# Spreading the four activations of a split piece over the steps, and putting GpSimd's reads of x2 first, in a two-layer convolution kernel

## The chip, the core and the metric

The kernel runs on one core of a Trainium2 chip. The metric is the device time of one execution in microseconds (us). Three runs of the kernel before gave 6400.53, 6409.91 and 6413.18 us, so its median is 6409.91 us. The profile comes from one more execution.

## The reference, cut to what matters

The input is four images of 96 channels and 128 x 128 pixels. A first layer (a state space scan) makes a new image `x`. The second layer, where the change lies, normalises each image and splits it at zero into a positive and a negative part:

```python
xr, x1, x2 = _relu_split_norm(x, sc1, sc2, res_coef, nc1, nc2)
y1 = NORM_SCALE * _layer_norm(_attn_conv(x1, x2, aw1, aw2, aw3))
y2 = NORM_SCALE * _layer_norm(_conv2d(x2, w_conv2, K // 2)) * x1
y = jnp.concatenate([y1, y2], axis=1)
return xr + _conv2d(y, w_full, 0) + b_full[None, :, None, None]
```

`_attn_conv` convolves x1 and x2 with 3 x 3 kernels into a key and a query, makes from their products (a softmax) the weights of one more 3 x 3 convolution per image, and applies it to a third convolution of x1, the value. All the images are independent in this layer.

## The kernel before, in words

**Stages.** Up to about 3600 us the first layer runs for all images, and image 0 passes its own split and its key, query, value and c2 convolutions (`direct_maps`, line 2126 on). After that, `attention` (line 1959) runs image by image on TensorE: for each strip of twelve rows it makes key, query, value and c2 (image 0 has them by then), then the attention weights (`weights`, line 1683), then the last convolution with those weights. This stream is called *left*. A second stream, *light*, prepares the next image and finishes the one before: `ssm_output`, then the split of image b+1, then `attn_output` of image b-1. `co_run` (line 302) pulls the two generators in turn by the costs that they yield, and so sets the order of emission.

**The order of the instructions.** In the stages after the scan nothing is pinned by hand: the Tile scheduler takes the emitted instructions, with their order of emission as priority, and writes one fixed order for each engine. Every engine then works through its own list in order. An instruction whose input is not there stops those behind it on its engine.

**The split.** `split_norm` (line 1101) reads an image in 16 pieces of 96 x 1024 pixels (tile `xn`). For images 1 to 3 (`planes` true) a piece has two sides, x1 and x2, and each side two halves of 512 pixels. For each half ScalarE writes scale*x + shift into a PSUM bank (line 1263), and VectorE multiplies it by the comparison of x with the threshold and writes it to SBUF, into the tile `half` (line 1267). The banks come from a pool of two that the light stream shares (`psr`), so the activation of one half can't start before VectorE has read the bank of two halves earlier.

**Steps.** `Later` (line 317) is a queue of closures with a count; each `tick` runs those whose count is 0 and lowers the others. A piece has six ticks, called steps here. Before, all four activations are emitted ahead of step 1, and the four VectorE operations in step 1. Then `planes_of` (line 1387) makes from each side six combinations of four neighbouring columns, the "planes", which the attention's Winograd-like products read. For x1 (`scaled`, line 1424) ScalarE makes two scaled copies, x4 (all columns, line 1428) and x2 (two column groups, line 1429; this x2 is a scratch tile, not the image part), in step 2; GpSimd combines them in ten operations (`differences`, line 1432, lines 1437 to 1442 and four of line 1406) in step 3; the store to memory (line 1450) is emitted in step 6. For x2 (`at_once`, line 1408) VectorE does it alone in step 5 with nine operations (lines 1413, 1414, 1418, two of 1420, four of 1406), and the store follows in step 6. The attention's value passes through the same `scaled` and `differences` (tile `own`), five or six rows at a time.

**Buffers.** x1 has two `half` tiles that alternate, x2 has one. In the split, x4 has two buffers and the scratch tile x2 one; the planes `pl` and `plv` have one each. `xn` has three.

**Other work named later.** Line 1477 and 1492 are the attention's matmuls; ScalarE copies their results out (`ends`, `odd`, line 1550), VectorE combines them (lines 1564 to 1572), and ScalarE copies shifted inputs (`yb`, line 1938) and transposed tiles (`kt`, line 1775). `weights` has the chain reduce (1697), exponential (1700), reciprocal and scaling (1701, 1702), transposes on TensorE (1711), copies (1712) and the combination of lines 1302 to 1308.

Of the kernel before, what the change touches and what calls it, by code (L numbers as in the profile page):

```python
# [11 lines left out]
AF = mybir.ActivationFunctionType  # L12
ALU = mybir.AluOpType
# [4 lines left out]
C = 96  # L18
# [14 lines left out]
TN = W // TW  # L33
# [38 lines left out]
def kernel(  # L72
# [26 lines left out]
    nc = tc.nc  # L99
# [193 lines left out]
    def part(ps, *shape):  # L293
        n = 1
        for d in shape[1:]:
            n *= d
        t = bank(ps)[: shape[0], :n]
        return t if len(shape) == 2 else t.rearrange("p (a b) -> p a b", b=shape[2])
# [802 lines left out]
    def split_norm(xnew, x1d, x2d, stats, keep, cnt, ps, side, planes, vector, done):  # L1101


        with ExitStack() as pools:
# [12 lines left out]
            a = col("rstd")  # L1117
            rsqrt(a, gs[:, 1:2])

            m = col("m1")  # L1120
# [19 lines left out]
            later = Later()  # L1140
# [58 lines left out]
            shift = kept[:, 0:2]  # L1199
            nc.vector.tensor_mul(shift, sa, navg)  # L1200
            scale = kept[:, 2:4]
# [18 lines left out]
            thr = kept[:, 8:9]  # L1220
# [4 lines left out]
            def stored(i, m, h):  # L1225
                if planes:
                    def then(pl):
                        store_planes(nc.sync, m, i * RS, RS, pl)
                        done[m is x2d] = (i + 1) * RS

                    return planes_of(later, p2, h, RS, then, vector=vector(i, m is x2d))
                at = (i * RS + 1) * PW
                return lambda: nc.scalar.dma_start(m[:, at : at + RS * PW], h)
# [8 lines left out]
            for i in range(NS):  # L1242
                y = ahead.pop(0)
                piece(i + 3)
                for side_, m in ((0, x1d), (1, x2d)):
                    op = ALU.is_le if side_ else ALU.is_gt
                    if planes:
                        h = half[side_][i % len(half[side_])]
                        v, to = (
                            t.rearrange("p (a b) -> p a b", b=b)[:, :, 0:TN]  # L1250
                            for t, b in ((y, TN), (h, PB))
                        )
                        k, parts = TW * R, 2
                    else:
                        h = p2.tile([C, RS * PW], F32, name=f"half{side_}", bufs=4)
                        hv = h.rearrange("p (h w) -> p h w", w=PW)
                        nc.gpsimd.memset(hv[:, :, 0:1], 0.0)
                        v, to = y.rearrange("p (h w) -> p h w", w=W), hv[:, :, 1:PW]
                        k, parts = RS, 1
                    for a in range(0, k * parts, k):  # L1260
                        x, o = v[:, a : a + k], to[:, a : a + k]
                        f = part(ps, C, k, TN) if planes else o
                        nc.scalar.activation(
                            f, x, AF.Identity,
                            scale=scale[:, side_ : side_ + 1], bias=shift[:, side_ : side_ + 1],
                        )
                        later(lambda o=o, x=x, f=f, op=op: nc.vector.scalar_tensor_tensor(
                            o, x, thr, f, op, ALU.mult
                        ))
                    later(stored(i, m, h), 1 + 3 * side_ * planes)  # L1270
                for _ in range(6 if planes else 1):
                    later.tick()
                    yield 2.5 if planes else 3.5
# [113 lines left out]
    def planes_of(later, pool, t, r, then, most=RS, vector=False, bufs=2, p=C, pb=PB, pp=PP):  # L1387

        a2 = AA * AA
        v = t[:, : r * pp].rearrange("p (h x) -> p h x", x=pp)
        over = pb - 1

        def planes(name, bufs):
            pl = pool.tile([128 if p < C else p, NP, most * TN], F32, name=name, bufs=bufs)[:p, :, : r * TN]
            return pl, [pl[:, i].rearrange("p (h t) -> p h t", t=TN) for i in range(NP)]

        def sums(eng, mid, outer, to):
            f1, f2 = mid[:, :, 0:TN], mid[:, :, pb : pb + TN]  # L1400
            f3, f0 = outer[:, :, 0:TN], outer[:, :, over:]
            for i, op, x, y in (
                (1, eng.tensor_add, f2, f1), (2, eng.tensor_sub, f2, f1),
                (0, eng.tensor_sub, f2, f0), (5, eng.tensor_sub, f3, f1),
            ):
                op(to[i], x, y)  # L1406

        def at_once():
            f = pool.tile([p, most, 6 * TN + 4], F32, name="diff", bufs=1)[:, :r]
            mid, outer, df = f[:, :, : 2 * PB], f[:, :, 2 * PB : 130], f[:, :, 130:]  # L1410
            pl, to = planes("plv", 1)
            stt = nc.vector.scalar_tensor_tensor
            stt(mid, v[:, :, : 2 * PB], -a2, v[:, :, 2 * PB :], ALU.mult, ALU.add)
            stt(
                outer, v[:, :, 2 * PB : 2 * PB + 2 * TN], -a2, v[:, :, 1 : 1 + 2 * TN],
                ALU.mult, ALU.add,
            )
            nc.vector.tensor_sub(df, v[:, :, 2 * PB :], v[:, :, : 2 * PB])
            for i, f in ((3, AA), (4, -AA)):
                stt(to[i], df[:, :, 0:TN], f, df[:, :, PB : PB + TN], ALU.mult, ALU.add)  # L1420
            sums(nc.vector, mid, outer, to)
            later(lambda: then(pl))

        def scaled():
            q = 128 if p < C else p
            x4 = pool.tile([q, most * JW], F32, name="x4", bufs=bufs)[:p, : r * pp]
            x2 = pool.tile([q, most, 2, PB], F32, name="x2", bufs=1)[:p, :r]
            nc.scalar.mul(x4, t[:, : r * pp], a2)
            nc.scalar.mul(x2, blocks(t, r, pp, 2 * pb, 2, PB), AA)
            later(lambda: differences(x4.rearrange("p (h x) -> p h x", x=pp), x2))  # L1430

        def differences(x4, x2):
            mid, outer = x4[:, :, : 2 * PB], x4[:, :, 2 * pb : 2 * pb + over + TN]
            d1 = x2[:, :, 0, 0:TN]
            pl, to = planes("pl", 1)
            sub, add = nc.gpsimd.tensor_sub, nc.gpsimd.tensor_add
            sub(mid, v[:, :, 2 * pb : 2 * pb + 2 * PB], mid)
            sub(outer, v[:, :, 1 : 1 + over + TN], outer)
            sub(to[4], v[:, :, 3 * pb : 3 * pb + TN], v[:, :, pb : pb + TN])
            sub(d1, x2[:, :, 1, 0:TN], d1)  # L1440
            add(to[3], to[4], d1)
            sub(to[4], to[4], d1)
            sums(nc.gpsimd, mid, outer, to)
            later(lambda: then(pl), 2)

        return at_once if vector else scaled
# [1075 lines left out]
    with tc.tile_pool(name="wp", bufs=1, side="left") as wp:  # L2522
# [7 lines left out]
        for images, pace in (([0], 0.25), ([1], 0.75), ([2, 3], 1.35)):  # L2530
            left = projections(images, weights, stats, wp, psl)
            if images[0] == 0:
                next(left)
                next(others)
                made = pair_weights()
                next(made)
                while ready[0] < 2:
# [3 lines left out]
                planes = [  # L2541
                    [new_planes(f"{n}{i}") for n in ("x1p", "x2p", "vp")] for i in range(2)
                ]
# [154 lines left out]
```

## Time and profile before

| what | value |
|---|---|
| median of three runs | 6409.91 us |
| the profiled execution | 6409.68 us |
| its span, first to last instruction | 6407.8 us, so 1.9 us lie around it |
| granted TensorE clock, mean | 0.902 |
| the split of image 1 | 3607 to about 3803 us, beside the end of image 0's maps and its last convolution |
| the split of image 2 | 4290 to 4570 us, beside the attention of image 1 |
| the split of image 3 | 5109 to 5405 us, beside the attention of image 2 |
| DMA, mean over the span | 188 GB/s |

The page of a profile gives for each engine its busy time and share. A view of windows gives the same for stretches of time. A line of the view of waits says who waited for whom: the sum in us, how often, the longest. A line of the timeline has the start in us, the duration in us, engine, line of the source, operation, output<-inputs, and in brackets the idle time of the engine before it with what ended it. PE is TensorE, PEld its weight loads, DVE VectorE, ACT ScalarE, POOL GpSimd; a q after the engine's name marks its sequencer, which waits or issues DMAs.

### The profile page before, as it was taken

Reading aid. Unit: us, or ns where it says so; the run is one execution under the profiler, and the core shown is the slowest. Engines: PE = TensorE matmul, PEld = TensorE weight load, DVE = VectorE, ACT = ScalarE, POOL = GpSimd, SP = SyncE. Lnnn points to the kernel's source line nnn. Section 1 sums busy time; section 2 is a strip of 40 time slices with the busy share of each in tenths; the row PEclk is TensorE's granted clock in tenths of the full one; section 3 lists DMA queues with packets and bytes.
Section 4 is the critical chain, followed back from the end, with each engine's and each line's share of the span. In section 5 each row is a group of like instructions: output and inputs, shape, how many; then the busy total and the mean of one; then the engine's idle time right before and its main releaser. Section 6 shows DMA issues by size and latency. Waiting matters only on the chain. (4 is left out here: it accounts for less than half of the span.)

```text
span 6407.8 us, 76468 instructions
## 1 busy us (share of the span) xinstructions
PE 5253.4 (82%) x23264; PEld 2254.8 (35%) x23264; DVE 4699.9 (73%) x7132; ACT 3759.4 (59%) x4770; POOL 3238.6 (51%) x2476
## 2 busy tenths in 40 slices
PE   6889988987888643989988588977888877889888
PEld 2333322322222111444433234345333444345553
DVE  4247878988989768989844686468774687988767
ACT  1247767787787666777622465466644665545642
POOL 1326757978879554979822234436304365022310
PEclk9899989998999765999999799989989888999989
DMA  6766777775675766676667686665776656967668
GB/s 155 175 160 189 198 199 199 214 221 163 198 202 171 202 183 207 196 213 179 182 185 195 166 228 163 195 169 156 214 199 184 175 149 165 245 167 180 191 168 221
DMA packets 897706, 1205.30 MB, mean 188 GB/s; under 512 B 230644, under 2 KB 745642, under 8 KB 884816
## 3 DMA queue, kind: packets, MB, share of 16 engines
q1 hardware_dynamic: 866640, 1145.36, 65.5%
q0 software_dynamic: 16336, 38.51, 2.3%
q10 hardware_dynamic: 14320, 16.54, 0.9%
q8 instruction: 187, 3.06, 0.2%
q14 instruction: 223, 1.83, 0.1%
HBM read 777.82 MB, written 345.62 MB: 175 GB/s over the span
## 5 line engine op out<-in xcount | busy, mean ns | idle before, releaser
L633 PE MATMUL bank<-y,wp 128*128 128x512 f32 (+3 forms) x3584 | 1310.9, 622 | 83.8 <-DMA y<-y 41.0
L866 POOL TENSOR_TENSOR y<-y,dl 128x1024 f32<-128x1024 f32 x384 | 1058.5, 2757 | 263.0 <-DVE dl L858 240.3
L833 POOL TENSOR_TENSOR dl<-dl,u 128x1024 f32<-128x1024 f32 x384 | 1008.8, 2627 | 253.1 <-ACT dA L809 121.1
L854 DVE TENSOR_TENSOR_SCAN dA<-dA,pBC 128x512 f32<-128x512 f32 x768 | 981.6, 1278 | 30.7
L2169 PE MATMUL bank<-y,wn 128*64 128x384 f32 (+5 forms) x2408 | 680.1, 507 | 58.3 <-DMA y<-x1d 34.1
L1477 PE MATMUL two<-ya,wd 128*64 128x192 f32 (+3 forms) x2376 | 582.2, 414 | 174.0 <-ACT odd L1550 65.1
L633 PEld LDWEIGHTS bank<-y,wp 128*128 128x128 f32 (+3 forms) x3584 | 456.2, 168 | 749.3 <-issue 651.1
L858 DVE TENSOR_TENSOR dl<-dA,pBC 128x512 f32<-128x512 f32 x768 | 528.5, 688 | 255.8 <-PE pBC L747 183.8
L747 PE MATMUL pBC<-xr,wbc 60*128 60x512 bf16 (+1 forms) x1536 | 457.8, 404 | 311.5 <-DVE dA L854 239.1
L1938 ACT COPY yb<-ya 64x768 f32<-64x768 f32 (+1 forms) x660 | 537.7, 815 | 195.5 <-PE two L1477 113.8
L676 ACT ACTIVATE dl<-pd,dtb 128x512 f32<-128x512 f32 x768 | 485.5, 684 | 187.9 <-PE pd L747 171.5
L1477 PE MATMUL two<-yb,wd 128*64 128x192 f32 (+3 forms) x2376 | 559.0, 400 | 4.0 <-ACT yb L1938 4.0
L837 DVE TENSOR_TENSOR pBC<-dl,pBC 128x512 f32<-128x512 f32 x768 | 527.5, 687 | 8.8 <-POOL dl L833 7.8
L2169 PEld LDWEIGHTS bank<-y,wn 128*64 128x64 f32 (+3 forms) x2408 | 310.3, 169 | 357.2 <-issue 186.2
L809 ACT ACTIVATE dA<-dl,negA 128x1024 f32<-128x1024 f32 x384 | 420.3, 1141 | 2.3
L1477 PEld LDWEIGHTS two<-ya,wd 128*64 128x64 f32 (+1 forms) x2376 | 262.2, 165 | 370.9 <-ACT odd L1550 75.0
L676 ACT ACT_TABLE_LOAD x248 | 318.2, 1283 | 91.9 <-PE pd L747 79.7
L747 PEld LDWEIGHTS <-wbc 60*128 60x128 bf16 (+1 forms) x1536 | 103.1, 96 | 752.1 <-issue 739.3
L1477 PEld LDWEIGHTS two<-yb,wd 128*64 128x64 f32 (+1 forms) x2376 | 289.7, 167 | 150.5 <-issue 42.1
L1477 PE MATMUL two<-ya,wa 128*96 128x384 f32 (+1 forms) x528 | 231.2, 521 | 72.9 <-DMA ya<-vp 27.0
L1550 ACT COPY odd<-two 128x384 f32<-128x384 f32 (+5 forms) x176 | 115.8, 658 | 291.3 <-PE two L1492 179.1
L1406 POOL TENSOR_TENSOR pl<-x 96x256 f32<-96x256 f32 (+3 forms) x396 | 275.2, 710 | 0.0
(322 smaller groups left out, 9105.4 us busy)
## 6 DMA issues: line engine op xcount, KB each, us to landing
u<-zb SPq DMA_DIRECT2D x192, 1024.0 KB
yms<-y SPq DMA_DIRECT2D x96, 512.0 KB
xn<-xnew SPq DMA_DIRECT2D x128, 384.0 KB
ya<-vp SPq DMA_DIRECT2D x120, 336.0 KB
y<-y SPq DMA_DIRECT2D x128, 258.2 KB
zb<-z SPq DMA_DIRECT2D x64, 512.0 KB
y<-yms SPq DMA_DIRECT2D x64, 512.0 KB
ya<-x1p SPq DMA_DIRECT2D x90, 336.0 KB
```

The costliest lines, as they stand in the source:

```text
L633: nc.tensor.matmul(blocks(pz[p:e]), lhsT=ws[k][:, d, c : c + e - p], rhs=window(ys[k], at, d, n), start=(i == 0), stop=(i == len(terms) - 1),)
L676: nc.scalar.activation(dst, src, AF.Softplus, bias=bias)
L747: nc.tensor.matmul(p, lhsT=w[rows], rhs=xr[rows, at : at + CH], start=True, stop=True)
L809: nc.scalar.activation(live[m]["dA"], live[m]["dl"], AF.Exp, scale=negA[:, g % 3, k : k + 1])
L833: nc.gpsimd.tensor_mul(t, t, u_view(n))
L837: nc.vector.tensor_mul(p, live[n]["dl"][:, bass.ts(half, CH)], p)
L854: nc.vector.tensor_tensor_scan(h, h, p, init, ALU.mult, ALU.add)
L858: nc.vector.tensor_mul(live[n]["dl"][:, sl], live[n]["dA"][:, sl], live[n]["C", half])
L866: nc.gpsimd.tensor_add(v, v, t.rearrange("p (a b) -> p a b", b=W))
L1477: nc.tensor.matmul(of(to[p:e], r), lhsT=w[:, i, c : c + e - p], rhs=tiles(t[k][PAIR[i]][:, SLOT[i]], o, r), start=(k == 0), stop=False,)
L1938: nc.scalar.copy(yb[k][64 * h - 64 : 64 * h, :, :n], ya[k][0:64, :, h * TN : h * TN + n])
L2169: nc.tensor.matmul(pc[p:e, :n].rearrange("p (h w) -> p h w", w=W), lhsT=w[:, c : c + e - p], rhs=v[:, :, 0:W], start=(i == 0), stop=(i == ...
```

## The change

In `split_norm` the activation of a half is put into a closure `made`. The first of a piece is emitted at once; the second, third and fourth are handed to `later`, so that they are emitted in steps 1, 2 and 3. Each closure queues its VectorE operation for the step after. The planes of x1 begin one step later (count 2 for 1), those of x2 in the same step as before (count 4). Image 0's split (`planes` false) has the turn 0 everywhere and keeps its order. In `differences` the same ten GpSimd operations are emitted in another order: the four that read the scratch tile x2 or feed those that do come first.

```diff
-                        f = part(ps, C, k, TN) if planes else o
-                        nc.scalar.activation(
-                            f, x, AF.Identity,
-                            scale=scale[:, side_ : side_ + 1], bias=shift[:, side_ : side_ + 1],
-                        )
-                        later(lambda o=o, x=x, f=f, op=op: nc.vector.scalar_tensor_tensor(
-                            o, x, thr, f, op, ALU.mult
-                        ))
-                    later(stored(i, m, h), 1 + 3 * side_ * planes)
+
+                        def made(x=x, o=o, op=op, side_=side_, k=k):
+                            f = part(ps, C, k, TN) if planes else o
+                            nc.scalar.activation(
+                                f, x, AF.Identity,
+                                scale=scale[:, side_ : side_ + 1],
+                                bias=shift[:, side_ : side_ + 1],
+                            )
+                            later(lambda: nc.vector.scalar_tensor_tensor(
+                                o, x, thr, f, op, ALU.mult
+                            ))
+
+                        turn = (2 * side_ + a // k) * planes
+                        if turn:
+                            later(made, turn - 1)
+                        else:
+                            made()
+                    later(stored(i, m, h), (2 + 2 * side_) if planes else 1)
...
             sub, add = nc.gpsimd.tensor_sub, nc.gpsimd.tensor_add
+            sub(d1, x2[:, :, 1, 0:TN], d1)
+            sub(to[4], v[:, :, 3 * pb : 3 * pb + TN], v[:, :, pb : pb + TN])
+            add(to[3], to[4], d1)
+            sub(to[4], to[4], d1)
             sub(mid, v[:, :, 2 * pb : 2 * pb + 2 * PB], mid)
             sub(outer, v[:, :, 1 : 1 + over + TN], outer)
-            sub(to[4], v[:, :, 3 * pb : 3 * pb + TN], v[:, :, pb : pb + TN])
-            sub(d1, x2[:, :, 1, 0:TN], d1)
-            add(to[3], to[4], d1)
-            sub(to[4], to[4], d1)
             sums(nc.gpsimd, mid, outer, to)
```

## The prediction

> **What bounds the kernel now.** I read the page first, then the windows of the three stages that the change touches, then the lines of the split, then the timeline around TensorE's longest gaps.
>
> ```profile
> span 6407.8 us, 76468 instructions
> PE 5253.4 (82%) x23264; PEld 2254.8 (35%) x23264; DVE 4699.9 (73%) x7132; ACT 3759.4 (59%) x4770; POOL 3238.6 (51%) x2476
> ```
>
> Over the whole span TensorE is the busiest engine. The windows show that this is not so where images 1, 2 and 3 are split (columns: stretch, its length, busy time and instructions of each engine, granted clock, DMA):
>
> ```profile
> 3600.00:3830.00 230.00, 158.01 (x551) 73.38 (x550) 200.74 (x349) 135.09 (x185) 100.29 (x126) 0.83 0.77 206
> 4290.00:4570.00 280.00, 219.72 (x1384) 131.47 (x1382) 237.72 (x448) 181.41 (x249) 170.77 (x244) 0.88 0.66 175
> 5109.00:5405.00 296.00, 234.49 (x1664) 153.45 (x1660) 246.51 (x454) 180.24 (x250) 189.80 (x268) 0.87 0.59 155
> ```
>
> In these 806 us VectorE (third busy figure) is at 83 to 87% and ahead of TensorE (first), which stands idle for 72, 60 and 62 us. What ends its waits there, in the view of waits of each window, is ScalarE for 32.5, 40.3 and 44.9 us (sum 117.7: the copies odd, ends, yb, kt) and VectorE for 12.3, 11.7 and 16.4 us (sum 40.4); in the first also one DMA wait of 27.0 us. The lines of the split:
>
> ```profile
> L1263 ACT ACTIVATE bank<-xn,kept x192: 759/775/787, 3606.8 to 5398.6; 96x512 f32<-96x512 f32 x192
>   DVE half L1267: 87.1, 43
> ...
> L1267 DVE SCALAR_TENSOR_TENSOR half<-xn,kept,bank x192: 723/736/764, 3607.6 to 5405.3; 96x512 f32<-96x512 f32 x192
>   POOL pl L1439: 25.9, 6
>   ACT bank L1263: 23.5, 17
> ```
>
> ScalarE stood idle 87.1 us, 43 times, before an activation whose bank VectorE had not yet read; 17.0, 29.8 and 36.5 us (83.3) of it lie in the three windows. The other direction, VectorE waiting for the activation, is 23.5 us. A wait, in the timeline:
>
> ```profile
> 4338.48 0.83 ACT L1938 COPY yb<-ya 64x768 f32<-64x768 f32 x1
> ...
> 4343.43 0.73 DVE L1267 SCALAR_TENSOR_TENSOR half<-xn,kept,bank 96x512 f32<-96x512 f32 x1
> ...
> 4344.20 0.78 ACT L1263 ACTIVATE bank<-xn,kept 96x512 f32<-96x512 f32 x1 [4.89 <-DVE half L1267]
> ```
>
> ScalarE did nothing for 4.89 us with a copy for TensorE (ends, at 4345.99) behind. Last, two seams, where the attention weights are made while a split is under way:
>
> ```profile
> 3652.95 1.64 PE L1711 MATMUL bank<-ident,sm 96*96 96x96 f32 x9 [9.76 <-DVE sm L1702]
> ...
> 3681.63 1.56 PE L1477 MATMUL two<-ya,wa 128*96 128x384 f32 x2 [27.04 <-DMA ya<-vp]
> ```
>
> ```profile
> 5406.38 1.34 DVE L2235 BATCH_NORM_AGGREGATE mv_a<-c2a 32x2 f32<-32x264 f32 x1
> ...
> 5414.88 0.15 DVE L1701 RECIPROCAL den<-den 96x1 f32<-96x1 f32 x1
> ...
> 5415.78 1.67 PE L1711 MATMUL two<-ident,sm 96*96 96x96 f32 x9 [1.20 <-DVE sm L1702]
> ...
> 5429.97 1.57 PE L1477 MATMUL two<-ya,wa 128*96 128x384 f32 x2 [9.98 <-DVE w L2267]
> ```
>
> At the first VectorE is busy nearly without a gap from 3640 to 3671, so each operation of the split in that queue delays TensorE's restart. At the second the exponential has ended at 5410.19, but the reciprocal runs at 5414.88, because the small operations of image 1's output (line 2235 and its like) stand ahead of it.
>
> [...] the 4.89 us above hold back ready work. [...] line 1267, one of whose inputs is in PSUM, stays at 723 to 764 beside GpSimd. So the moved VectorE operation keeps its length wherever it lands.
>
> **The change, part by part.** No instruction is added or removed; only orders change. So I compared the orders that the scheduler wrote for the two programs.
>
> *GpSimd's ten operations.* In none of the 48 groups of the split do the x2 operations come first in the new program. 37 groups have one and the same order in both (lines 1437, 1438, 1440, 1439, then 1406 and the others in turn): x4 is made first, so its readers are ready first. ScalarE's waits for the scratch tile (line 1429 for line 1442: 45.0 us over the kernel) stay. Cost 0; if a reordering came after all, it could return at most those 45.0 times 0.38 (below), 17 us.
>
> *The activations.* ScalarE's waits come from those placed directly behind the VectorE operation that frees their bank. Matching the 186 that have a predecessor two halves back to the trace: the 53 with no other ScalarE instruction between waited 1.42 us on average (75.5 in all), the other 133 only 0.09. The new order has 37 and 149: 37 x 1.42 + 149 x 0.09 = 66, against 88, so 22 us of waits go, not 87. The scheduler had spread the four before, since it too waits for the bank. What replaces them: the VectorE operation is now more often next in its own queue after its activation was placed. The 15 with no VectorE instruction between waited 1.15 us each, the others 0.04. The new order has 35 and 157: 35 x 1.15 + 157 x 0.04 = 46.5 us, against 24, so 22 us are added.
>
> *What passes to TensorE.* The waits of TensorE for ScalarE are 117.7 us against 309 of ScalarE's idle time in the windows (94.9 + 98.6 + 115.8): 0.38. For VectorE 40.4 against 121 (29.3 + 42.3 + 49.5): 0.33. Spreading evenly is my choice. Saved 22 x 0.38 = 8; added 22 x 0.33 = 7. Both ends for the added part: 0 (hidden) and 22 (all passes). Queued behind the waiting VectorE operation are the combinations of lines 1564 to 1572, and matmuls wait for those.
>
> *Seams.* At the first, the new VectorE order has 78 instructions, not 83, from the split's start to the store of the weights: three of line 1267 (0.74) and two of the planes' (0.7) fewer, 3.6 us. They come later, beside the last convolution, where image 1 isn't needed yet. At the second, the new order has none of the small output operations between reduce and reciprocal: 5414.88 - 5410.2 = 4.7 us. They stall TensorE later instead (2.88 and 2.28 us before lines 202 and 2241 now), so I count half, 2.4. The middle seam has the same counts. Sum -6.
>
> *What else moves.* The planes of x1 start a step later (277 us / 96 steps = 2.9 us), and their store falls into the next piece, on SP's queue behind x2's store and the next load of xn. From store to GpSimd's next use of pl it is three steps as before, so GpSimd's waits for that store (26.8 us in the second window) stay: 0. The last reader of xn is up to 3 steps, 9 us, later, and the load into its buffer is three pieces, 52 us, ahead of use: 0, and if SP did hold, the attention's ya loads are behind, now two strips ahead. VectorE's wait for GpSimd's reading of an older half (25.9 us) has a step less: 0 to 6 times 2.9 times 0.33, 6 us; I take 0, as program order shows no closer pair.
>
> **Sum.** -8 + 7 - 6 = -7: 6409.7 - 7 = 6403 us. The profiled execution is 0.2 us under the median, so no correction.
>
> **Rivals.** *The waits vanish* (B): on the chip a step of 2.9 us is longer than activation plus multiplication (1.5 us), so all 83 us go and VectorE gains none. Worth 83 x 0.38 = 32, with the seams 38: 6372 us. For it speaks that an activation is now emitted a step after its bank's reader; against it, 37 of 53 close pairs remain. *VectorE takes the wait over* (C): it is the fullest engine of these windows, so what it idles is not made up; all 22 us reach TensorE, ScalarE's relief ends in other waits, and the seams' work is paid for later: 6409.7 + 22 = 6432 us, slower. It decides once more than (8 + 6) / 22 = 0.64 of the added waits pass. *Nothing moves* (D): TensorE's order differs only in some 3% of its rows, mostly swaps, and the scheduler undoes the edit as for GpSimd: 6410 us.
>
> **Chances.** A (6403, own range 6390 to 6416) 0.42, B 0.25, C 0.25, D 0.08. A change of 0.2%, 12.8 us, is about what a measurement of this kernel can tell from none. Faster than that: 0.3 of A and nine tenths of B, 0.35. Slower: most of C and a trace of A, 0.23. Same: the rest, 0.42. The range, 6370 to 6431, reaches to B and nearly to C; the cut is in the tails beyond them.
>
> **What would show it.** Right: the idle time before the activation falls from 87 to 60 to 75 us while VectorE's before the multiplication rises from 23.5 to over 40; GpSimd's groups as before; the 27.0 us gap starts its last convolution some 4 us sooner; the reciprocal of image 2 follows the exponential. B: the 87 falls below 30, TensorE's waits for ScalarE below 90. C: the windows' VectorE idle time grows by 20 us or more and TensorE's with it. I am wrong altogether if the difference lies outside 3600 to 5450 us, or comes from DMA waits of ya.

## The result, and the profile after

The changed kernel takes 6422.9 us (median of 22 runs, 6399.45 to 6438.67). The kernel before, run beside it, takes 6388.06 us (22 runs, 6370.76 to 6413.18). The ratio is 1.005, 95% interval 1.0039 to 1.0061: the change costs 0.5%, some 32 us. The forecast was 6403 us against 6409.91, no measurable change. The median of before in these runs is 22 us below that of the three runs shown ahead of the prediction, so what is compared from here on are ratios of runs made side by side.

The profiled execution of before, on which the prediction rests, was one of the longer ones (6409.68 us); the one of after has 6415.16 us. So their spans show only 5.5 us of the 32. I profiled each kernel once more (e1, e2 below), and every stage below is given from both executions.

The engines' row of the page after, then the three windows of the split (columns as before):

```profile
span 6413.3 us, 76436 instructions
...
PE 5255.4 (82%) x23264; PEld 2256.7 (35%) x23264; DVE 4695.8 (73%) x7132; ACT 3759.2 (59%) x4770; POOL 3247.4 (51%) x2476
```

```profile
3600.00:3830.00 230.00, 155.52 (x535) 72.81 (x533) 195.81 (x326) 140.03 (x190) 99.84 (x123) 0.85 0.75 204
4290.00:4570.00 280.00, 212.50 (x1266) 127.74 (x1267) 223.03 (x415) 164.96 (x227) 160.59 (x229) 0.84 0.60 164
5109.00:5405.00 296.00, 231.26 (x1658) 148.32 (x1654) 238.37 (x443) 176.34 (x247) 193.10 (x267) 0.88 0.55 151
```

The busy times of the whole are those of before, within 0.3%: no work was added. In the second window every engine does less in the same 280 us (TensorE 212.50 for 219.72, VectorE 223.03 for 237.72, GpSimd 160.59 for 170.77), the DMA moves 164 GB/s for 175, and the granted clock is 0.84 for 0.88. The windows are fixed in time, and in this execution the split of image 2 starts 16 us earlier, so part of the difference is other work. The lines of the split after:

```profile
L1265 ACT ACTIVATE bank<-xn,kept x192: 760/774/787, 3598.1 to 5411.1; 96x512 f32<-96x512 f32 x192
...
  DVE half L1270: 66.7, 26
```

```profile
L1270 DVE SCALAR_TENSOR_TENSOR half<-xn,kept,bank x192: 712/737/762, 3598.9 to 5414.0; 96x512 f32<-96x512 f32 x192
...
  ACT bank L1265: 74.6, 50
  POOL pl L1447: 13.7, 5
```

ScalarE's idle time before the activation fell from 87.1 to 66.7 us; the prediction had worked out 66. VectorE's before the multiplication rose from 23.5 to 74.6 us; the prediction had 46.5. The durations are the same: 774 ns in the median for the activation and 737 for the multiplication, before 775 and 736. TensorE's restart at the first seam, in the timeline:

```profile
3638.40 1.67 PE L1720 MATMUL bank<-ident,sm 96*96 96x96 f32 x9 [10.59 <-DVE sm L1711]
...
3659.75 1.57 PE L1486 MATMUL two<-ya,wa 128*96 128x384 f32 x2 [19.68 <-DMA ya<-vp]
...
3687.47 1.57 PE L1486 MATMUL two<-ya,wa 128*96 128x384 f32 x2 [5.71 <-DMA ya<-vp]
```

The gap of 27.04 us is now 19.68, but 28 us later stands a wait of 5.71 us that was not there. The time went into the last convolutions. I take a seam from the first transpose of the weights to the first matmul that reads them (`wa`), and a last convolution from there to its last such matmul. In us, two executions each:

| stretch | before | after | TensorE idle before | after |
|---|---|---|---|---|
| image 0: seam | 28.7, 27.9 | 21.4, 21.2 | 27.0, 26.2 | 19.7, 19.5 |
| image 0: last convolution | 144.3, 140.4 | 156.5, 156.5 | 20.7, 20.1 | 32.1, 35.6 |
| from the split of image 2 to the seam of image 1 | 198.9, 199.2 | 209.5, 212.0 | 45.2, 44.8 | 53.6, 53.6 |
| image 1: last convolution | 130.0, 130.1 | 140.5, 140.0 | 11.7, 11.3 | 19.0, 19.9 |
| image 2: seam and last convolution | 195.6, 196.2 | 200.3, 201.6 | 26.8, 26.7 | 30.7, 31.0 |

With the means: -7 + 14 + 12 + 10 + 5 = 34 us. Ahead of the first seam another 5 us are saved: from its 50th matmul before the first transpose to that transpose, TensorE takes 29.2 and 29.3 us, before 34.3 in both executions. That leaves 29 us. Of the other stretches, the seam of image 1 is 0.7 us longer, and those beside splits differ by no more than executions of one kernel do. What follows the last convolution of image 2 holds no split; it takes 803.4 and 800.7 us after 796.5 and 792.8 before, with 2 us more idle time and a granted clock of 0.92 for 0.93. Experiments with and without the change range there from 791 to 806 us, so I put this on neither side.

### The profile page after: what moved, and what is told of

It reads as the page before. It is cut to its first block, busy times and chain, and to the rows that moved or that the text cites. A ratio compares the mean times of both kernels' runs of the same rounds, so it can differ in the third digit from the quotient of the medians.

```text
span 6413.3 us, 76436 instructions
## 1 busy us (share of the span) xinstructions
PE 5255.4 (82%) x23264; PEld 2256.7 (35%) x23264; DVE 4695.8 (73%) x7132; ACT 3759.2 (59%) x4770; POOL 3247.4 (51%) x2476
## 5 line engine op out<-in xcount | busy, mean ns | idle before, releaser
L633 PE MATMUL bank<-y,wp 128*128 128x512 f32 (+3 forms) x3584 | 1310.6, 621 | 80.9 <-DMA y<-y 40.4
L854 DVE TENSOR_TENSOR_SCAN dA<-dA,pBC 128x512 f32<-128x512 f32 x768 | 981.7, 1278 | 30.7
L1415 POOL TENSOR_TENSOR pl<-x 128x192 f32<-128x192 f32 (+3 forms) x396 | 289.3, 745 | 0.2
```

The lines of the kernel that those rows point to most:

```text
L633: nc.tensor.matmul(blocks(pz[p:e]), lhsT=ws[k][:, d, c : c + e - p], rhs=window(ys[k], at, d, n), start=(i == 0), stop=(i == len(terms) - 1),)
L854: nc.vector.tensor_tensor_scan(h, h, p, init, ALU.mult, ALU.add)
```

## The experiments

The theories were: the added VectorE waits carry the loss (rival C of the prediction); or the step by which x1's planes and their store were put off, which the prediction had put at 0.

**Both kernels again (e1, e2), and GpSimd's order alone (e3).** The kernel before and the changed one, executed once more each; then the kernel before with only this:

```diff
+            sub(d1, x2[:, :, 1, 0:TN], d1)
+            sub(to[4], v[:, :, 3 * pb : 3 * pb + TN], v[:, :, pb : pb + TN])
+            add(to[3], to[4], d1)
+            sub(to[4], to[4], d1)
             sub(mid, v[:, :, 2 * pb : 2 * pb + 2 * PB], mid)
             sub(outer, v[:, :, 1 : 1 + over + TN], outer)
-            sub(to[4], v[:, :, 3 * pb : 3 * pb + TN], v[:, :, pb : pb + TN])
-            sub(d1, x2[:, :, 1, 0:TN], d1)
-            add(to[3], to[4], d1)
-            sub(to[4], to[4], d1)
```

> The kernel before, unchanged, for a second profile: how far do two profiles of one program differ, stage by stage? The profile on record lies some 20 us above the median of its 22 runs. Both theories: its activations wait near 87 us for VectorE and VectorE near 24 us for them, as in the first profile, since the order is the same. If these two sums differ by more than 15 us between two profiles of one program, neither can carry an explanation of 32 us.

> The changed kernel, unchanged, for a second profile. Theory 1 (VectorE took the wait over): VectorE's waits for the activation stay near 75 us, and the last convolutions of images 0 and 1, which run beside a split, stay longer than in the kernel before by about 10 us each (156 and 140 us against 144 and 130). Theory 2 (the later planes of x1 hold back loads): the same lengths, but with TensorE's waits for loads of the attention in front. If the two lengths fall back to those of the kernel before, the lengths are chance.

> Only the new order of GpSimd's ten operations, the activations as before. The scheduler's orders of the four other engines are those of the kernel before to the last row, GpSimd's differ in 20 of 2474. Theory 1 and 2: no change, ratio 1.000 within 0.001. If it is over 1.002, GpSimd's few moved rows carry part of the loss.

Measured: spans 6384.1 and 6434.4 us. The waits in the split repeat: 79.8 us (ScalarE) and 21.0 (VectorE) in e1, 65.1 and 76.9 in e2, each within 7.3 us of the first execution. e3: 1.0009 (0.9999 to 1.0019). The order of GpSimd is worth nothing, as predicted; the loss is in the other part.

**The planes of x1 late, without moving an activation (e4).** The kernel before with one count:

```diff
-                    later(stored(i, m, h), 1 + 3 * side_ * planes)
+                    later(stored(i, m, h), (2 + 2 * side_) if planes else 1)
```

> All four activations at once as before, but the planes of x1 (two scaled copies, ten GpSimd operations, the store) one step later, as in the changed kernel. Theory 1: no loss, ratio 1.000 within 0.0015, and VectorE's waits for the activation stay near 24 us. Theory 2: most of the loss, ratio 1.003 to 1.005.

Measured: 1.0053 (1.0039 to 1.0067), as much as the whole change. VectorE's waits for the activation in the split rise to 58.9 us though no activation was moved, so most of that rise does not come from moving them.

**One image at a time (e5, e6, e7), and two activations at once (e8).** The change of the activations and of the planes' step for one image alone; then turns 0, 0, 2, 2 with the planes of x1 in their old step. All four keep GpSimd's old order.

```diff
-                        turn = (2 * side_ + a // k) * planes
+                        turn = (2 * side_ + a // k) * spread
...
-                    later(stored(i, m, h), (2 + 2 * side_) if planes else 1)
+                    later(stored(i, m, h), (1 + spread, 4)[side_] if planes else 1)
...
-                self.done,
+                self.done, int(self.b == 1),
```

```diff
-                        turn = (2 * side_ + a // k) * planes
+                        turn = 2 * side_ * planes
...
-                    later(stored(i, m, h), (2 + 2 * side_) if planes else 1)
+                    later(stored(i, m, h), 1 + 3 * side_ * planes)
```

> The activations spread over the steps for image 1 alone (beside the end of image 0's maps and its last convolution), images 2 and 3 as before, GpSimd's order as before. Theory 1: a loss in proportion to the VectorE waits that the split of one image gains: about a third, 1.001 to 1.002. If the loss comes from one place alone, one of the three single runs has all of it and two have none.

> The same for image 2 alone (beside the attention of image 1). Theory 1: 1.001 to 1.002, with VectorE's waits for the activation up in the second window alone. The profile pair of before and after lost most here, some 19 us between 4415 and 4590 us, so a theory of one place expects 1.003 here.

> The same for image 3 alone (beside the attention of image 2). Theory 1: 1.001 to 1.002. A theory of one place in image 2's window: 1.000.

> Two activations at once and two steps later the other two, each pair's multiplications in the step after; all other work in the steps of the kernel before. A pair fills the two banks, so no activation stands behind a bank that is not yet due. Theory 1: the ScalarE waits fall as in the changed kernel (below 70 us), and the time follows VectorE's waits for the activation: no loss if they stay near 24 us, a loss of 0.3 to 0.5% if they reach 60. Theory 2: no loss, since the planes are on time.

Measured: 1.0007 (0.9996 to 1.0019), 1.0025 (1.0016 to 1.0034), 1.005 (1.0032 to 1.0067), 1.0034 (1.0021 to 1.0046). The first three don't add up (0.82% against 0.5%), but each lengthens the last convolution beside its own split and leaves the others alone, as the table further down shows. For e7 that is 10 of its 32 us; another 18 lie beside the split itself, from its first activation to the seam (323.3 us, before 306.3 and 303.1). The 0.34% of e8 fits neither theory: its planes and their store are on time, and VectorE waits only 32.0 us for the activations.

**The store one step earlier in the changed kernel (e9), one step later in the kernel before (e10).** Only the store of x1's planes moves; `bufs` is 2 in the split.

```diff
-            later(lambda: then(pl), 2)
+            later(lambda: then(pl), 1 if bufs == 2 else 2)
```

```diff
-            later(lambda: then(pl), 2)
+            later(lambda: then(pl), 3 if bufs == 2 else 2)
```

> The changed kernel, with the store of x1's planes emitted two steps after GpSimd's operations and not three, so that it falls into step 6 of its own piece again, as before the change; everything else late as in the changed kernel. Theory 2a (the store's place is the loss: it stands in the next piece, behind the load of xn, and GpSimd's single pl waits for it): the loss goes, ratio under 1.002, GpSimd's waits for the store back from 140 to about 90 us. Theory 2b (the scaled copies and GpSimd's operations themselves are too late in the piece): ratio stays at 1.004 to 1.006.

> The kernel before, with only the store of x1's planes one step later, so in the next piece's step 1. Theory 2a: 1.003 to 1.005, GpSimd's waits for the store 125 us or more. Theory 2b: under 1.002. Theory 1 (VectorE's waits): 1.000, since no activation moves.

Measured: e9 1.0019 (1.0009 to 1.003), e10 1.0062 (1.005 to 1.0074). One store, moved over the end of its piece with no compute operation touched in the source, costs more than the whole change; taken back over it, it returns some 0.3%.

In the program that the scheduler writes, much more than the store has moved. I compared the orders in the traces row by row, by source line, tile and shape. The two executions of before agree on ScalarE, VectorE, GpSimd and SP to the last row. In e10 another instruction stands at 564 of ScalarE's 4770 places, 1114 of VectorE's 7132, 379 of GpSimd's 2476, 281 of SP's 5986, and 1190 of TensorE's 23264 (28 between the two executions of before). e4 and e10 differ from each other in 32, 51, 23, 13 and 22 places: the two edits end in nearly the same program. In the last convolution of image 1 and in that of image 2 with its seam, e3, e8, e9 and e16 have TensorE's order of before in every row; the changed kernel, e4 and e10 differ from it in 34 to 56 of 413 rows and in 74 to 88 of 535.

SP's queue in the last convolution of image 1, in the timeline of before:

```profile
4526.17 0.56 SPq L1450 DMA_DIRECT2D x1p<-pl  x1
4526.82 0.59 SPq L1450 DMA_DIRECT2D x2p<-plv  x1
...
4532.05 0.38 SPq L1111 DMA_DIRECT2D xn<-xnew  x1
```

The same in that of after:

```profile
4530.37 0.56 SPq L1459 DMA_DIRECT2D x2p<-plv  x1
...
4532.94 0.63 SPq L1111 DMA_DIRECT2D xn<-xnew  x1
4533.66 0.56 SPq L1459 DMA_DIRECT2D x1p<-pl  x1
```

And in that of e10:

```profile
4541.43 0.56 SPq L1450 DMA_DIRECT2D x2p<-plv  x1
4544.29 0.41 SPq L1111 DMA_DIRECT2D xn<-xnew  x1
4544.80 0.56 SPq L1450 DMA_DIRECT2D x1p<-pl  x1
```

Before, the store of x1's planes goes first and the next load of xn last; in the other two it goes behind that load. Over the three splits the changed kernel issues it behind x2's store in 44 of 48 pieces, and in 31 behind the load too; e10 in 45 and 30; the kernel before in none. GpSimd, with one `pl` buffer, waits for this store to end. Its line in the view of waits, before:

```profile
POOL pl L1439 <- DMA x1p<-pl: 90.4, 11, 20.0
```

After:

```profile
POOL pl L1447 <- DMA x1p<-pl: 138.9, 19, 21.1
```

In e9:

```profile
POOL pl L1447 <- DMA x1p<-pl: 124.2, 17, 19.0
```

The second executions have 89.2 and 140.7 us, e10 has 132.0. But e9, expected at 90, has 124.2, and e16 and e8 have 119.8 and 119.2, all three with the store in its piece. So this wait doesn't tell long last convolutions from short ones.

**Two buffers for `pl` (e11 changed, e12 before), and for the scratch tile x2 (e13 changed, e14 before).** Each is paid for with one xn buffer in these splits, e11 and e12 with one strip of `ya` as well.

```diff
-            p4 = pools.enter_context(tc.tile_pool(name="n4", bufs=3, side=side))
+            p4 = pools.enter_context(tc.tile_pool(name="n4", bufs=2 if planes else 3, side=side))
...
-            pl, to = planes("pl", 1)
+            pl, to = planes("pl", bufs)
...
-            ya = self.p2.tile([128, 2, (AR + 2) * TN], F32, name="ya", bufs=8)
+            ya = self.p2.tile([128, 2, (AR + 2) * TN], F32, name="ya", bufs=7)
```

```diff
-            p4 = pools.enter_context(tc.tile_pool(name="n4", bufs=3, side=side))
+            p4 = pools.enter_context(tc.tile_pool(name="n4", bufs=2 if planes else 3, side=side))
...
-            x2 = pool.tile([q, most, 2, PB], F32, name="x2", bufs=1)[:p, :r]
+            x2 = pool.tile([q, most, 2, PB], F32, name="x2", bufs=bufs)[:p, :r]
```

> The changed kernel with two buffers of the split's pl in place of one, so that GpSimd needn't wait for the store; for the room, xn has two buffers in place of three there and the attention's ya seven in place of eight. To be read against the next run, which does the same to the kernel before. Theory 2 (the loop pl, store, pl sets the split's pace): GpSimd's waits for the store near 0, the piece of image 2 back to 21.5 us from 23.4, and no more than 0.2% between the two. Theory 1: the difference stays at 0.4 to 0.6%.

> The kernel before with the same buffers: two pl, two xn, seven ya. Theory 2: no slower than the kernel before, and up to 0.3% faster if the 90 us of GpSimd's waits mattered there too, unless the missing ya buffer costs. It is the base for the run before.

> The changed kernel with two buffers for the scratch tile x2 in the split (one of its three xn buffers in the split of images 1 to 3 is given up for the room). Theory now (the late store holds GpSimd, and ScalarE's in-order queue stops at the copy into the single x2): ScalarE's waits for GpSimd before the scaled copies fall from 49 us to below 15, the activations' followers on VectorE wait less (below 50, from 75), and most of the 32 us loss goes: 1.001 +-0.002 times the kernel before. Rival (the waits for GpSimd are only a sign; the loss lies in the activations' own order): still 1.005. Rival (with two buffers for xn the next load is late): slower, above 1.006, with waits for DMA ahead of the activations.

> The kernel before with the same two edits, to price the room given up. If the theory holds, 26 us of waits for GpSimd go to below 8 and the time is 0.998 to 1.001. If the third xn buffer matters: 1.004 or more, and then the run before is to be read against this one.

Measured: e11 1.007 (1.0058 to 1.0082), e12 1.0105 (1.0088 to 1.0121); e13 1.0142 (1.0128 to 1.0156), e14 1.004 (1.0027 to 1.0053). The second buffer of `pl`, with the room given up for it, costs more than it returns, but with it the changed kernel is the faster of the two. Its last convolution of image 1 is then 135.5 us against 133.8, where one buffer had 140 against 130; image 0's with its seam stays longer, 184.4 us against 177.2. e13 ended a theory of mine. Over ten runs ScalarE's waits for GpSimd before its scaled copies had followed the ratio best (26 us before, 50 after, 64 in e4 and in e10), and I held that ScalarE stood at the single x2 with the activations queued behind. Its copy into x2, from the line's own view in the changed kernel:

```profile
L1438 ACT ACTIVATE x<-half x48: 639/657/662, 3601.7 to 5425.5; 96x528 f32<-96x528 f32 x48
...
  POOL pl L1449: 60.4, 20
```

The same line in e13:

```profile
L1438 ACT ACTIVATE x<-half x48: 640/643/665, 3619.1 to 5506.2; 96x528 f32<-96x528 f32 x48
...
  POOL pl L1449: 16.9, 4
```

The line counts the attention's copies too; of those in the split 3.0 us are left from 49.7. Yet e13 is 1.0% above e14, and its last convolution of image 1 is 140.0 us as in the changed kernel. The waits followed the loss and did not carry it.

**The store earlier in the kernel before (e15), and the activations at steps 0, 0, 1, 2 with planes and store in their old steps (e16).** e15 is the kernel before with the edit of e9. e16 has GpSimd's old order and:

```diff
-                        turn = (2 * side_ + a // k) * planes
+                        turn = (side_ + side_ * (a // k)) * planes
...
-                    later(stored(i, m, h), (2 + 2 * side_) if planes else 1)
+                    later(stored(i, m, h), 1 + 3 * side_ * planes)
```

> The kernel before with only the store of x1's planes one step earlier (two steps after GpSimd's operations instead of three), the activations all at once as before. If the place of the store carries the loss, an earlier one may still gain: 0.998 to 1.000. If the scheduler's order already lets it go as soon as GpSimd is done: 1.000 with the same waits. If SP stops at the store that waits for GpSimd and holds the loads behind: 1.002 or more.

> The activations emitted at steps 0, 0, 1 and 2 instead of 0, 1, 2, 3, so that x1's planes and their store stay at their old step while x2's activations are spread as in the change. If spreading itself costs nothing and the late store is the cause: 0.999 to 1.001. If spreading costs by itself (VectorE waits for the activation): 1.002 to 1.005, with VectorE's wait above 50 us. If spreading gains once the store is on time: below 0.998.

Measured: e15 1.0067 (1.0053 to 1.0081), e16 1.0031 (1.0017 to 1.0045). Earlier is no better than later. By its time e15 is the third case expected, but SP stands no longer at x1's store beside the split of image 2 (10.7 us, before 10.8 and 10.3). It loses elsewhere, too: its last convolutions are near those of before, and the 470 us between the last convolution of image 0 and the split of image 2 are 21 us longer (485.1 for 465.3 and 462.2); there TensorE's order differs from before in 635 of 2358 rows. e16 shows that spreading the activations gains nothing with the store on time; its cost was expected to come with VectorE's waits above 50 us, but they are 31.2.

**The store taken from SP's queue (e17 changed, e18 before).** The store of x1's planes is issued by GpSimd itself, behind the operations that make them.

```diff
-                        store_planes(nc.sync, m, i * RS, RS, pl)
+                        store_planes(nc.gpsimd if m is x1d else nc.sync, m, i * RS, RS, pl)
```

> The changed kernel with the store of x1's planes issued from GpSimd's own queue, right behind the ten operations that make them, and no longer from SP's queue, where it stands behind the next load. If the loss comes from the store's place on SP's queue: the last convolution of image 1 falls from 140 us to 134 or less, that of image 0 with its seam from 178 to 172, and the time to within 0.2 % of the same edit on the kernel before (1.002 or less between the two). If the planes' operations on GpSimd being a step later carry it, wherever the store is issued: the last convolutions stay at 140 and 178 us and the two differ by 0.4 to 0.6 %. If issuing from GpSimd costs it time by itself, both are slower by the same.

> The kernel before with the store of x1's planes issued from GpSimd's queue. SP holds that store 6 to 8 us after GpSimd is done. If GpSimd's wait for it (90 us over the three splits) is worth something: 0.996 to 0.999. If issuing takes GpSimd's time, or the load of xn now goes ahead of the store: 1.002 or more. It is the base that e17 is read against.

Measured: e17 1.0021 (1.0011 to 1.0032), e18 1.0053 (1.004 to 1.0066). Off SP's queue the change costs nothing: it is then 0.3% the faster. The last convolution of image 1 is short in both, 125.7 and 125.8 us; that of image 0 with its seam, expected at 172, stays at 181.0 and 178.1. Both are slower than the kernel before, whose splits take less time beside the attention (the stretch of image 2: 199 us before, 222.5 in e17, 242.4 in e18).

The three places, by whether the split beside them has x1's store in its own piece (on time) or a step behind it (late), for the kernels with unchanged buffers and the store on SP's queue (us, from the trace; where a kernel has two executions, both):

| split | image 0: seam and last convolution | image 1: last convolution | image 2: seam and last convolution |
|---|---|---|---|
| on time: before | 173.0, 168.3 | 130.0, 130.1 | 195.6, 196.2 |
| on time: e3, e9, e16, e8, e15 | 174.0, 170.8, 171.8, 175.5, 166.5 | 131.8, 131.1, 133.2, 132.2, 134.0 | 195.7, 195.7, 195.8, 195.8, 196.9 |
| on time: the two other images of e5, e6, e7 | 170.6 (e6), 170.2 (e7) | 130.0 (e5), 128.4 (e7) | 195.9 (e5), 195.3 (e6) |
| late: after | 177.9, 177.7 | 140.5, 140.0 | 200.3, 201.6 |
| late: e4, e10 | 178.1, 176.0 | 142.0, 142.7 | 205.2, 200.6 |
| late: the image of e5, e6, e7 | 180.4 (e5) | 143.0 (e6) | 205.7 (e7) |

No late figure lies in the range of those on time, in any column; in the first the margin is only 0.5 us, where two executions of before differ by 4.7. With the means of before and after that is 7 + 10 + 5 = 22 of the 34 us, or 17 of the 29 that are left with the 5 us saved ahead of the first seam. The last convolution of image 1, in the view of windows, before:

```profile
4502.30:4632.30 130.00, 118.26 (x413) 50.75 (x413) 107.75 (x207) 84.05 (x110) 40.48 (x58) 0.96 0.82 222
```

After:

```profile
4497.10:4637.60 140.50, 121.51 (x412) 52.02 (x412) 110.58 (x201) 81.59 (x107) 45.80 (x61) 0.93 0.72 201
```

In e10:

```profile
4507.90:4650.60 142.70, 121.16 (x412) 52.74 (x412) 110.52 (x200) 81.59 (x107) 46.69 (x61) 0.90 0.72 201
```

In e9:

```profile
4491.50:4622.60 131.10, 119.02 (x413) 50.85 (x413) 111.08 (x207) 84.06 (x110) 41.44 (x58) 0.95 0.81 223
```

After (activations moved, store late) and e10 (none moved, store late) are alike, down to ScalarE's 107 and GpSimd's 61 instructions: more of the split's tail lies beside the convolution (its last activation starts 81 and 79 us after the convolution does, before 65), the DMA moves 201 instead of 222 GB/s, and TensorE idles 19 to 21.5 us instead of 12. e9 (moved, store on time) is like before. The rest of the lengthening is TensorE's busy time, 121.5 and 121.2 us for 118.3, at a granted clock of 0.93 and 0.90 for 0.96.

## Why the prediction was wrong, step by step

The decisive runs stand in four cells, as ratios to the kernel before:

| | store in its own piece | store a step later, in the next piece |
|---|---|---|
| activations at once | 1, 1.0067 (e15, a step earlier) | 1.0062 (e10), 1.0053 (e4, planes too) |
| activations spread | 1.0019 (e9, planes a step later), 1.0031 (e16, one step less spread), 1.0034 (e8, two and two) | 1.005 (the change) |

- **"What else moves", the step that failed.** The prediction saw the store fall into the next piece, behind x2's store and the load of xn, and put it at 0, since "from store to GpSimd's next use of pl it is three steps as before". So it named the queue, but priced it by counting steps in the source, and it left out that the scheduler would write other orders around a later store. With no activation moved, the store's step costs 0.62%, 40 us (e10), and with the planes 0.53%, 34 us (e4). GpSimd's waits for the store, forecast to stay, went from 90 to 139 us. TensorE's idle time in the three windows is 193.8 and 196.3 us before, 206.7 and 208.6 after, 212.0 in e10 and 201.8 in e4, but 193.2 in e9 and 190.6 in e16: it rises with the late store and not with the spread. A case in the trace of after: SP issued nothing from 4411.69 to 4419.13, where x1's store went 0.02 us after GpSimd's last operation on its planes, and the loads of `ya` that stand behind it followed at 4419.82. In the window of image 2 SP stood at x1's store until GpSimd was done for 17.2 and 22.0 us after and 28.4 in e10, before for 10.8 and 10.3. Over the three windows together, though, it stood there no longer than before (50.2 and 54.7 us, before 53.3 and 47.2), so the length of this wait is not the loss.
- **GpSimd's order, 0: right.** 1.0009, with 1 inside the interval.
- **The activations: the waits right on one side, the effect near.** ScalarE's 66 us were worked out and 66.7 measured. VectorE's 46.5 became 74.6. Most of the rise comes with the late store: 58.9 us in e4 and 59.6 in e10, none of whose activations are moved, but 31.6 in e9 and 31.2 in e16, with the store on time. In their effect, -8 + 7 = -1 us was forecast. The columns of the table give +0.2 and +0.3% with the store on time (12 to 20 us), and no loss with it late (1.005 against 1.0053 and 1.0062). So the term is small in both, though with the store on time it is a cost of its own.
- **What passes to TensorE.** By the prediction its waits for ScalarE in the three windows were to fall from 117.7 by 8 us, and those for VectorE to rise from 40.4 by 7. They are 125.9 and 44.8 us (124.4 and 46.1 in e2). With the store on time they are 115.0 and 43.9 in e9, 115.4 and 41.8 in e16, no further from before than its own second execution (111.8 and 45.4). So no run confirms the shares of 0.38 and 0.33. The wait that the prediction showed also held back less than it said. In the timeline of before the matmuls whose result `ends` copies are these, and TensorE's wait for the copy follows:

```profile
4342.88 0.91 PE L1492 MATMUL two<-ya,wd 32*128 32x384 f32 x4
...
4346.82 0.91 PE L1477 MATMUL two<-ya,wd 128*128 128x384 f32 x2 [0.25 <-ACT ends L1550]
```

The matmuls end at 4343.79, so the copy's input was ready only for the last 0.41 of ScalarE's 4.89 us, in which it stood behind the activation that has its place ahead of it (4344.20, the copy 4345.99), and TensorE lost 0.25.

- **Seams, -6: right in kind, given back.** The first seam gained 7 us, and 5 more ahead of its first transpose (3.6 forecast); e5, e8, e9 and e16 have both, e4 and e10 neither, so this is the spread's doing. The prediction let the work that left it "come later, beside the last convolution" at no cost. In e9 and e16, with the store on time, seam and last convolution together are 170.8 and 171.8 us, before 173.0 and 168.3: the 7 us came back, part as a new wait for `ya` (5.71 us after, 5.77 in e9). At the second seam the reciprocal follows the exponential as forecast, but by the late store: from the end of the exponential to the first transpose it is 1.0 us after and in e4 and e10, 5.6 before, 6.3 in e9 and e16. And the last convolution starts no sooner:

```profile
5407.47 1.01 ACT L1709 ACTIVATE sm<-sm,mx 96x864 f32<-96x864 f32 x1
...
5408.60 0.16 DVE L1710 RECIPROCAL den<-den 96x1 f32<-96x1 f32 x1 [2.57 <-ACT sm L1709]
...
5409.61 1.65 PE L1720 MATMUL two<-ident,sm 96*96 96x96 f32 x9 [6.06 <-DVE sm L1711]
...
5426.13 1.57 PE L1486 MATMUL two<-ya,wa 128*96 128x384 f32 x2 [11.92 <-DVE so L197]
```

From the first transpose to the first such matmul it is now 16.5 us, before 14.2: the small output operations that left the front stand behind.

- **The signs.** All that the prediction named for being right came true: 66.7 and 74.6 us, GpSimd's groups, the first gap 7 us shorter, the reciprocal. They were signs of orders and waits, and none of them was about the store.
- **Rival C** had side and size (6432 us, +22), and its sign came: in the windows VectorE's idle time grew by 28 us and TensorE's by 13. Two of its parts held, ScalarE's relief ended in other waits and the first seam's 7 us were paid for later. Its main term did not: TensorE's waits for VectorE grew by 4 us and not 22, and VectorE's own waits rise nearly as far in e10 (59.6 us), where no activation is moved.

Is there a gain under the loss? Three pairs have the same edit of the store or its buffer on both sides (intervals joined in quadrature): e17 to e18 0.9968 (0.9951 to 0.9985), e11 to e12 0.9965 (0.9945 to 0.9986), e9 to e15 0.9952 (0.993 to 0.997). In these the change gains 0.3 to 0.5%. Against that stands e13 to e14, 1.0102 (1.008 to 1.012). With unchanged buffers and the store late on both sides, the change to e10 is 0.9988 (0.997 to 1.0004). And the bases of all these pairs are slower than the kernel before. So the spread of the activations has no fixed value; it depends on what else is late.

**What stays open.** That the step of the store, and not that of the planes or the activations, makes the last convolutions long is shown at the level of the source: e10 has them long with everything else in its old step, e9 short with everything else late. What carries it in the written program is not shown. The store's place on SP's queue is one candidate; the orders of the other engines, which change with it, are the other, and no run moves one without the other. e17 doesn't settle it, since its orders change as well.

ScalarE's stop at x2 is ruled out, and GpSimd's waits for the store do not separate the kernels. For image 1 two things speak for the queue and the single `pl`: in its last convolution SP stands at x1's store for 3 to 6 us in the changed kernel, e4 and e10 and not at all in before, e9 and e16, and in e11 neither this wait nor most of the lengthening is there. For the last convolutions of images 0 and 2, where SP stands there 1.4 us at most, nothing of the kind was found. What TensorE waits for in the last convolution is spread over `odd`, `ends`, `own` and `ya`, none of them over 4 us more than before. The 12 us beside the attention of image 1 are not separated into causes; they appear in e4, e6 and e10 (208.7, 208.9, 210.7 us), but also, smaller, in e16, e8 and e15 (207.6, 206.2, 206.3). Why an earlier store costs in e15, and why e13 loses so much, I did not find. None of the edited kernels beat the kernel before, and a store moved either way loses 0.6%: its order may simply be a good one that most edits spoil. That is a guess.

## What to carry to other kernels

A step in the source that only moves an issue of a DMA is a change of that queue's order, and where a scheduler writes the orders, of all the others too (in e10 281 places of SP's 5986, and 1114 of VectorE's 7132). Compare the written order of every engine, and write down what stands ahead of it on the queue before and after, at the end of a loop's turn above all, and who waits for its buffer. Price the moved compute and the moved issue as two edits, and run each alone. A wait that follows the loss over many runs is not its cause until it has been taken away and the loss with it.

## What the runs showed of the hardware that was not expected

One and the same convolution ran at different granted clocks. In the last convolution of image 1 it was 0.96 in both executions of before, with 11.7 and 11.3 us of idle time on TensorE; 0.93 and 0.94 in those of after, with 19.0 and 19.9; 0.90 in e10, with 21.5. TensorE's busy time was 118.3 and 118.8, 121.5 and 120.1, and 121.2 us. In these five executions the clock is lower where the idle time is 19.0 us or more than where it is 11.7 or less. The sum of the idle time alone doesn't give it, though: e17 has 0.91 with 8.7 us and e18 0.92 with 10.6, but e16 0.95 with 13.1. What does is not shown. And a DMA that GpSimd issues takes time on its queue: in the timeline of e17 from 4400 to 4440 us each of the two issues lasts 0.70 us, with 0.30 us of idle time ahead of it, and GpSimd's next operation starts 0.73 and 0.63 us after the issue did. The second of them:

```profile
4411.59 1.23 POOL L1415 TENSOR_TENSOR pl<-x 96x256 f32<-96x256 f32 x2
4413.12 0.70 POOL L1459 DMA_DIRECT2D x1p<-pl  x1 [0.30 <-POOL pl L1415]
```
